# An attention block on one core: the triangular inverse laid out over all row groups of the array, its tiles in three sets, and a reciprocal in two halves

## The chip, the cores and the metric

The kernel runs on one core of a Trainium2 chip. A core has five engines that run side by side, each in the order of its own program: PE (TensorE: matmuls into PSUM, with its weight loads shown apart as PEld), DVE (VectorE), ACT (ScalarE), POOL (GpSimd), and SP (SyncE), which here only issues DMA transfers. The metric is the device time of one execution in microseconds (us). Three runs of the kernel before took 3192.85, 3196.23 and 3197.49 us.

## The reference

Input x is 4 x 512 x 512 in f32 (4 batches, 512 tokens, 512 channels). Two layers are added to it. The first is a gated recurrence over tokens (called wkv below) whose result feeds a gated delta-rule attention with 16 query/key heads and 32 value heads of 128; the second is another wkv, followed by a 512 x 512 product with a binarized weight:

```python
x = x + attn(wkv(x, fside, fside, w1, u1, cond), W_qkvz, W_ba, conv_w, dt_bias, A_log, norm_w, W_out)
x = x + ffn(wkv(x, fside, fside, w2, u2, cond), weight, bias)
```

Of wkv, what matters here is its end, in which a forward and a backward scan over the tokens are divided by each other:

```python
num = nf + nb - ekv + euk * vf
den = df + db - ek + euk
base = sigmoid(r) * (num / maximum(den, 1e-08))
```

Of the attention, what matters is the inverse of a triangular matrix for each chunk of tokens and each value head, and its use:

```python
M = where(stril, einsum('bhncd,bhnmd->bhncm', k_beta, k) * decay, 0.0)
T = solve_triangular(eye + M, eye, lower=True)
v_c = einsum('bhnij,bhnjd->bhnid', T, v_beta)
```

The kernel computes this with chunks of 128 tokens, so that T is a 128 x 128 matrix, and a unit of work has 8 of them.

## The kernel before, in words

**Units.** The attention is cut into 64 units, one for each batch and query/key head (`unit`, L164: batch `n // 16`, head `n % 16`). A unit has two value heads and four chunks of 128 tokens, so NM = 8 triangular matrices. Weights come from HBM raw in the first batch, are turned on PE and stored for the three other batches.

**The plan.** The main loop runs once for each unit, and in each iteration goes through a list of 22 places (`plan`, L1027 to L1097), counted here from 0 to 21. Each place names a few steps and the unit that each is for, relative to the iteration: F is the iteration's own unit (projection, convolution, inverse), C the one before it (the chunk recurrence), O the one before that (norm of the output, turning), W the one before that (the product with W_out), and K the one that is six ahead (its keys, and the triangular matrix itself). Every instruction is kept in program order on its engine, so the order of this list is the order on each engine and in SP's queue of DMA issues.

**The recurrence** of unit C takes four rounds through the places: `chunk_r` (PE, tile ps_s, from the state), `chunk_r_end` (DVE, tile r), `chunk_w` (PE, tile ps_w, from r and the inverse), `chunk_w_end` (ACT, tile wd), `chunk_t` (PE, tiles ps_st and ps_o), `chunk_t_end` (DVE, tiles state and o). The fourth round has `chunk_r` at place 16, `chunk_w` at place 18 and `chunk_t` at place 20.

**The inverse.** The diagonal 32 x 32 blocks of each triangular matrix are inverted by substitution on POOL, four units at a time (`group_load`, `group_step`, `group_end`; the last stores them to HBM as `blocks_n` and, turned, as `blocks_t`, at place 13 of every fourth iteration). `inverse_load` (L651) brings a unit's blocks back into two tiles: `inv_t`, 128 partitions x 8 matrices x 128, which becomes the turned inverse, and `inv_n`, 64 partitions x 8 x 96. There are two sets of these tiles, used in turn, so the load for unit F + 1 stands behind the last `chunk_w` of unit C, at place 20. It is 7 DMA issues. Four steps on PE then put the off-diagonal blocks together, each followed by a copy from PSUM on DVE:

- step 1, `inverse_1` at place 2: 16 products of 32 x 32 blocks. The operands stand in partitions 32 to 63 or 96 to 127; the results go to PSUM partitions 0 to 31 or 32 to 63. The copy makes tile nv, 64 x 256.
- step 2, `inverse_2` at place 4: 24 products of 32 x 32 blocks, with operands in partitions 0 to 31, 32 to 63 and 0 to 31 in turn, and results in partitions 0 to 31, 64 to 95 and 32 to 63. Three copies of 32 x 256 put them into `inv_t` and `inv_n`.
- step 3, `inverse_3` at place 8: 8 products of 64 x 64 blocks, operands in partitions 64 to 127, results in 0 to 63. The copy makes tile nw, 64 x 512.
- step 4, `inverse_4` at place 10: 8 products of 64 x 64 blocks, operands and results in partitions 0 to 63. One copy of 64 x 512 into `inv_t`.

A product takes its row group of the array from the partitions of its operands, and its column group from the partitions of its result. All four steps, and also `key_pairs` (tile ps_kk, place 16) and `queries` (tile ps_kq, place 20), use the one PSUM bank with the tag "inv": each has to wait until what was in the bank has been read. For `queries` this is the end of `key_matrix` (L588; DVE, tile dkd, four operations at place 17 and four at place 18). In the profile a product of f32 shows as two matmul rows, so step 1 has 32 of them, step 2 has 48, and steps 3 and 4 have 16 each; ps_i is the tile of steps 1 and 3, ps_j that of steps 2 and 4.

**The wkv pieces.** The wkv of later batches, and all of the second wkv, are cut into 28 pieces of 128 channels x 512 tokens. A piece rides along in an iteration (steps named "wkv" in the plan), in those whose unit has the head 3, 4, 5 or 7 (first wkv, batches 0 to 2, for the batch to come) and 9, 11, 12 or 13 (second wkv, all batches). `wkv_over` (L291) is one reciprocal of 128 x 512 on DVE at place 15, ahead of `chunk_r_end` of the fourth round; `wkv_end` (L294) at place 18 uses it, and in the second wkv issues a store (`base2`). At head 8 of the first three batches the gates of the next batch are computed.

**SP's queue** from place 15 on: the load of `wo`, the store of `base2` where there is one, the load for the matrix of unit K + 1 (tile dkd), a weight load, the four stores of `key_blocks` (`blocks_m`), the seven of `inverse_load`, the load of tile dkt, and the next weights.

Before the loop, `inverse_load` is called for units 0 and 1 (L1317, L1318); iteration 0 leaves it out (L1409).

Of the kernel before, what the change touches and what calls it, by code (L numbers as in the profile page):

```python
# [9 lines left out]
F32 = mybir.dt.float32  # L10
# [6 lines left out]
P = 128  # L17
EPS = 1e-6

BS = 32  # L20
# [20 lines left out]
def kernel(  # L41
# [21 lines left out]
    B, S, D = x.shape  # L63
# [29 lines left out]
    def bank(tag, name):  # L93
        return pp.tile([P, 512], F32, tag=tag, name=name, bufs=banks[tag])
# [10 lines left out]
        out=tri_le, in_=tri_le, compare_op=ALU.is_ge, fill=0.0, base=0,  # L105
# [5 lines left out]
        out=tri_gt, in_=tri_gt, compare_op=ALU.is_gt, fill=0.0, base=0,  # L111
# [5 lines left out]


    inv_t, inv_n = [], []
    for i in range(2):  # L120
        t = const.tile([P, NM, P], F32, name=f"inv_t{i}")
        G.memset(t, 0.0)
        inv_t.append(t)
        t = const.tile([2 * BS, NM, 3 * BS], F32, name=f"inv_n{i}")
        G.memset(t, 0.0)
        inv_n.append(t)

# [4 lines left out]
    nw = const.tile([P, 1], F32, name="nw")  # L132
# [10 lines left out]
    blocks_n = dram.tile([NG, GROUP, NB, NM, BS, BS], F32, name="blocks_n")  # L143
    blocks_t = dram.tile([NG, GROUP, NB, NM, BS, BS], F32, name="blocks_t")

    with ExitStack() as main:
# [9 lines left out]
        u1p = main.enter_context(tc.tile_pool(name="u1", bufs=1))  # L156
# [7 lines left out]
        def unit(n):  # L164

            return (*divmod(n, HQ), units.setdefault(n, {}))
# [4 lines left out]
        for cb in range(KT):  # L171
            at = slice(cb * P, (cb + 1) * P)
# [472 lines left out]

        b0, b1, b2, b3 = (slice(d * BS, (d + 1) * BS) for d in range(NB))
        lo, hi = slice(0, 2 * BS), slice(2 * BS, 4 * BS)

        def inverse_load(n):  # L651
            b, hq, u = unit(n)
            Tt, Tn = u["Tt"], u["Tn"] = inv_t[n % 2], inv_n[n % 2]
            g, i = divmod(n, GROUP)
            for d, at in enumerate((b0, b1, b2, b3)):
# [12 lines left out]
        def inverse_1(n):  # L668
            b, hq, u = unit(n)
            M, Tt = u["d"], u["Tt"]  # L670
            ps = u["i"] = by_matrix(f"ps_i_{n}")
            for m in range(NM):
                for to, up, dn in ((b0, b0, b1), (b1, b2, b3)):
                    T.matmul(
                        ps[to, m, :BS], lhsT=M[dn, m, up], rhs=Tt[dn, m, dn], start=True, stop=True
                    )

        def inverse_1_end(n):
            b, hq, u = unit(n)
            u["nv"] = u1p.tile([2 * BS, NM, BS], F32, tag="nv", name=f"nv_{n}")  # L680
            V.tensor_copy(u["nv"], u["i"][lo, :, :BS])
# [13 lines left out]

        def inverse_2_end(n):
            b, hq, u = unit(n)
            Tt, Tn, ps = u["Tt"], u["Tn"], u["i"]
            V.tensor_copy(Tt[b2, :, b3], ps[b2, :, :BS])
            V.tensor_copy(Tn[b1, :, b0], ps[b1, :, :BS])  # L700
            V.tensor_copy(Tt[b0, :, b1], ps[b0, :, :BS])

        def inverse_3(n):
            b, hq, u = unit(n)
            ps = u["i"] = by_matrix(f"ps_i4_{n}")
            for m in range(NM):
                T.matmul(
                    ps[lo, m, :], lhsT=u["d"][hi, m, lo], rhs=u["Tt"][hi, m, hi],
                    start=True, stop=True,
                )  # L710

        def inverse_3_end(n):
            b, hq, u = unit(n)
            u["nw"] = u1p.tile([2 * BS, NM, 2 * BS], F32, tag="nw", name=f"nw_{n}")
            V.tensor_copy(u["nw"], u["i"][lo])

        def inverse_4(n):
            b, hq, u = unit(n)
            ps = u["i"] = by_matrix(f"ps_j4_{n}")
            for m in range(NM):  # L720
                T.matmul(
                    ps[lo, m, :], lhsT=u["Tn"][:, m, lo], rhs=u["nw"][:, m, :], start=True, stop=True
                )

        def inverse_4_end(n):
            b, hq, u = unit(n)
            V.tensor_copy(u["Tt"][lo, :, hi], u["i"][lo])


        def turn(n, r):  # L730
# [287 lines left out]
        def last_add(b, c):  # L1018
# [7 lines left out]
        K, F, C, O, W = AHEAD, 0, -1, -2, -3  # L1026
# [87 lines left out]
        for pool, tag, count, shape in (  # L1114
# [3 lines left out]
            for i in range(count):  # L1118
                t = pool.tile(shape, F32, tag=tag, name=f"lent_{tag}_{i}")
# [6 lines left out]
        for pool, tag, shape in ((u1p, "nz", [P, NC, 2, HD]), (u1p, "hT", [P, 2, S])):  # L1126
            t = pool.tile(shape, F32, tag=tag, name=f"lent_{tag}")
# [65 lines left out]
        for cb in range(KT):  # L1193
            w = wkv_start(0, 0, cb)
# [24 lines left out]
        ps = bank("pj", "ps_wba")  # L1219
# [9 lines left out]
        g = {"b": 0}  # L1229
# [122 lines left out]
        for b in range(B - 1):  # L1352
            i = at + 2 + 2 * b
# [98 lines left out]
```

## Time and profile before

| | us |
|---|---|
| median of three runs (lowest, highest) | 3196.23 (3192.85, 3197.49) |
| profiled execution, its own time | 3197.57 |
| its span, first to last instruction | 3195.8 |
| PE busy | 3069.3 (96%) |
| DVE busy | 2044.6 (64%) |
| ACT busy | 1861.6 (58%) |
| POOL busy | 1329.4 (42%) |

What follows is worked out with the profiled execution. In a row of the groups of instructions stand the engine, the operation, the tile written and those read, rows times columns of the array for a matmul, the size out and in, and the count; behind the first bar the group's busy time in us and the mean duration in ns; behind the second bar the idle time of the engine just before them, and what ended it. In the chain of waits a row has a start, a length, and the engine with its tile. Matmuls overlap one another, so the length of a stretch of them is read from start to start, or from the chain, and not from single durations.

### The profile page before, as it was taken

How to read it: one execution, taken by the hardware profiler on the slowest of the kernel's cores; microseconds unless marked ns; L12 is line 12 of the kernel's file. 1: busy time of each engine (PE TensorE's matmuls, PEld its weight loads, DVE VectorE, ACT ScalarE, POOL GpSimd, SP SyncE). 2: the span in 40 equal slices, each digit the busy share in tenths (PEclk: the TensorE clock that was granted, in tenths of full speed). 3: DMA queues.
4: the chain of work that ended last, by engine and by line, in shares of the span. 5: the costliest groups of instructions: out<-in, count | busy, mean ns of one | idle time of the engine just before them, and what ended most of it. 6: DMA issues, size and time to landing. Idle time of an engine off the chain costs nothing.

```text
span 3195.8 us, 57474 instructions
## 1 busy us (share of the span) xinstructions
PE 3069.3 (96%) x20058; PEld 2055.2 (64%) x20058; DVE 2044.6 (64%) x4454; ACT 1861.6 (58%) x5115; POOL 1329.4 (42%) x3042
## 2 busy tenths in 40 slices
PE   6489999999999999999999999999999999999998
PEld 3356766666766666666666666666666666665664
DVE  7545767666655776667655686667755656577542
ACT  2446666666666666556565666556666555655542
POOL 3216354263522646264432646255442515255302
PEclk9689999999999999999999999999999999999999
DMA  3334444444434323332332323323332332333321
GB/s 74 95 87 130 141 127 119 124 125 128 132 109 142 115 59 106 86 96 78 108 102 78 116 86 83 111 77 95 112 92 76 104 86 86 105 90 93 105 83 53
DMA packets 418800, 320.49 MB, mean 100 GB/s; under 512 B 217104, under 2 KB 326160, under 8 KB 418128
## 3 DMA queue, kind: packets, MB, share of 16 engines
q1 hardware_dynamic: 414288, 314.72, 33.6%
q8 instruction: 160, 2.62, 0.3%
q10 hardware_dynamic: 4224, 2.10, 0.2%
q14 instruction: 128, 1.05, 0.1%
HBM read 246.19 MB, written 70.52 MB: 99 GB/s over the span
## 4 chain that ended last, share of the span: by engine, by line
PE 80%; DVE 11%; ACT 3%; DMA 3%; issue 1%; SPq 1%; ACTq 0%; POOL 0%; DVEq 0%; POOLq 0%
PE ps_p L80 24%; PE ps_out L80 12%; PE ps_z L80 12%; PE ps_w L80 4%; PE ps_s L80 4%; PE ps_i L80 3%; PE ps_o L80 3%; PE ps_j L80 3%; DVE y L80 3%; PE ps_st L80 2%; PE ps_kq L80 2%; PE ps_f L80 2%; DVE f L80 2%; PE ps_h L80 1%; PE ps_v L80 1%
## 5 line engine op out<-in xcount | busy, mean ns | idle before, releaser
L80 PE MATMUL ps_p<-cT,w 128*128 128x512 f32 x2000 | 956.4, 606 | 8.4 <-ACT w L80 8.4
L80 DVE SCALAR_TENSOR_TENSOR y<-ps_p,cw,y 128x511 f32<-128x511 f32 (+2 forms) x768 | 570.9, 743 | 419.3 <-ACT y L80 405.6
L80 PEld LDWEIGHTS ps_p<-cT,w 128*128 128x128 f32 x2000 | 346.9, 191 | 302.0 <-issue 270.8
L80 PE MATMUL ps_z<-w,cT 128*128 128x256 f32 x2048 | 476.5, 379 | 0.0
L80 PE MATMUL ps_out<-wo,hT 128*128 128x512 f32 x1024 | 466.8, 599 | 7.3 <-DMA wo<-wosc 7.3
L80 PEld LDWEIGHTS ps_z<-w,cT 128*128 128x128 f32 x2048 | 373.7, 190 | 42.5
L80 PEld LDWEIGHTS ps_out<-wo,hT 128*128 128x128 f32 x1024 | 186.0, 191 | 195.8 <-issue 189.0
L80 POOL TENSOR_TENSOR L<-L,t 128x30 f32<-128x30 f32 (+14 forms) x450 | 270.4, 601 | 35.3
L80 ACT ACT_TABLE_LOAD x137 | 175.8, 1283 | 154.0 <-DVE y L80 116.0
L80 ACT ACTIVATE qs<-ps_s,eg 128x128 f32<-128x128 f32 x384 | 120.5, 366 | 229.5 <-DVE r L80 121.9
L80 POOL TENSOR_TENSOR t<-L 128x30 f32<-128x30 f32 (+14 forms) x450 | 228.7, 508 | 34.5 <-DMA L<-blocks_m 3.3
L80 POOL TENSOR_TENSOR rs_t_o<-rs_y_o 128x8 f32<-128x8 f32 x192 | 38.5, 201 | 461.0 <-DVE rs_y_o L80 450.0
L80 ACT ACTIVATE y<-ps_p,cw 128x512 f32<-128x512 f32 x256 | 174.1, 680 | 90.2 <-PE ps_p L80 90.1
L80 POOL TENSOR_SCALAR_AFFINE_SELECT dkd<-dkd 128x1024 f32<-128x1024 f32 x64 | 70.5, 1101 | 350.4 <-DMA dkd<-gsc 223.0
L80 ACT ACTIVATE dkt<-dkt,gsum 128x128 f32<-128x128 f32 x512 | 162.9, 392 | 69.3 <-POOL dkt L80 68.9
L80 DVE TENSOR_TENSOR x<-x,ps_out 128x512 f32<-128x512 f32 x256 | 168.9, 679 | 32.8 <-PE ps_out L80 32.6
L80 POOL TENSOR_TENSOR rs_t_k<-rs_y_k 128x4 f32<-128x4 f32 x174 | 48.3, 277 | 328.4 <-DVE rs_y_k L80 319.3
L80 DVE SCALAR_TENSOR_TENSOR o<-o,rs_y_o,nz 128x128 f32<-128x128 f32 x512 | 183.0, 412 | 0.1
L80 DVE SCALAR_TENSOR_TENSOR r<-ps_s,nbe,vb 128x128 f32<-128x128 f32 x384 | 115.9, 343 | 96.8 <-PE ps_s L80 96.7
L80 ACT ACTIVATE junk<-o 128x128 f32<-128x128 f32 x512 | 158.0, 309 | 31.8 <-DVE o L80 23.6
L80 DVE TENSOR_TENSOR o<-ps_o,qs 128x256 f32<-128x256 f32 x192 | 80.8, 421 | 144.1 <-PE ps_o L80 136.1
L80 ACT ACTIVATE wd<-ps_w,eg 128x128 f32<-128x128 f32 x384 | 119.7, 364 | 87.8 <-PE ps_w L80 87.5
(270 smaller groups left out, 5771.3 us busy)
## 6 DMA issues: line engine op xcount, KB each, us to landing
w<-wsc SPq DMA_DIRECT2D x288, 256.0 KB, 5.3
dkd<-gsc SPq DMA_DIRECT2D x64, 512.0 KB, 4.7
dkt<-gsc SPq DMA_DIRECT2D x64, 512.0 KB, 4.5
wraw<-in_L_attn_W_qkvz_dram SPq DMA_DIRECT2D x96, 256.0 KB, 3.0
wo<-wosc SPq DMA_DIRECT2D x96, 256.0 KB, 3.8
wsc<-w SPq DMA_DIRECT2D x90, 256.0 KB, 2.1
blocks_m<-dkd SPq DMA_DIRECT2D x256, 32.0 KB, 1.7
L<-blocks_m SPq DMA_DIRECT2D x16, 512.0 KB, 5.5
```

The costliest lines, as they stand in the source:

```text
L80: return lambda *args, **kw: tc.keep_in_program_order(op(*args, **kw))
```

## The change

Five edits, of which the first is the core.

1. The products of the inverse are spread over the array. Matrices 0 to 3 and 4 to 7 form two halves. A list `in_turn` takes a matrix of each half alternately, and the half selects the partitions of the results: 0 to 31 and 32 to 63 for one, 64 to 95 and 96 to 127 for the other in step 1; 0 to 63 and 64 to 127 in steps 3 and 4. In steps 2 and 4 the operands follow their half too. In step 2 the three kinds of products stand one kind after the other (all eight of the first, then of the second, then of the third) where they stood matrix by matrix. The number of products stays.
2. The copies from PSUM follow. nv is 128 x 128 in place of 64 x 256; step 2 is followed by six copies of 32 x 128 in place of three of 32 x 256; nw is 128 x 256 in place of 64 x 512; step 4 is followed by two copies of 64 x 256 in place of one of 64 x 512.
3. `inv_n` is laid out by halves, 128 partitions x 4 x 96, so its loads are six of half the size in place of three: `inverse_load` has 10 DMA issues in place of 7.
4. There are three sets of `inv_t` and `inv_n` in place of two, and `inverse_load` of F + 1 moves from place 20 to place 16, ahead of the store of `base2`, the dkd load and the `key_blocks` stores in SP's queue.
5. `wkv_over` does half of the 512 tokens at a time: the first half at the end of place 16, behind `chunk_r_end` and the taps, the second at the end of place 17, behind the first four operations of `key_matrix`. It stood at place 15.

```diff
-    for i in range(2):
+    for i in range(3):
         t = const.tile([P, NM, P], F32, name=f"inv_t{i}")
...
-        t = const.tile([2 * BS, NM, 3 * BS], F32, name=f"inv_n{i}")
+        t = const.tile([P, NM // 2, 3 * BS], F32, name=f"inv_n{i}")
...
-        def wkv_over(w):
-            V.reciprocal(w["df"], w["df"])
+        def wkv_over(w, half):
+            den = w["df"][:, half * S // 2 : (half + 1) * S // 2]
+            V.reciprocal(den, den)
...
+        HM = NM // 2
+        in_turn = [(h * HM + m, h, m) for m in range(HM) for h in range(2)]
...
-            Tt, Tn = u["Tt"], u["Tn"] = inv_t[n % 2], inv_n[n % 2]
+            Tt, Tn = u["Tt"], u["Tn"] = inv_t[n % 3], inv_n[n % 3]
...
-                    Q.dma_start(
-                        out=Tn[b1 if d else b0, :, at],
-                        in_=blocks_n[g, i, d].rearrange("m i j -> i m j"),
-                    )
+                    for h in range(2):
+                        Q.dma_start(
+                            out=Tn[blocks[2 * h + (d > 0)], :, at],
+                            in_=blocks_n[g, i, d, h * HM : (h + 1) * HM].rearrange("m i j -> i m j"),
+                        )
...
-            for m in range(NM):
-                for to, up, dn in ((b0, b0, b1), (b1, b2, b3)):
+            for m, h, mh in in_turn:
+                for up, dn, to in ((b0, b1, 2 * h), (b2, b3, 2 * h + 1)):
                     T.matmul(
-                        ps[to, m, :BS], lhsT=M[dn, m, up], rhs=Tt[dn, m, dn], start=True, stop=True
+                        ps[blocks[to], mh, :BS], lhsT=M[dn, m, up], rhs=Tt[dn, m, dn],
+                        start=True, stop=True,
                     )
...
-            for m in range(NM):
-                for to, at, col in ((b0, b0, b0), (b2, b1, b2)):
-                    T.matmul(
-                        ps[to, m, :BS], lhsT=Tn[at, m, col], rhs=nv[at, m, :], start=True, stop=True
-                    )
-                T.matmul(
-                    ps[b1, m, :BS], lhsT=nv[b0, m, :], rhs=Tn[b0, m, b0], start=True, stop=True
-                )
+            for what in range(3):
+                for m, h, mh in in_turn:
+                    at, dn = blocks[2 * h], blocks[2 * h + 1]
+                    if what == 0:
+                        to, lhsT, rhs = ps[at, mh], Tn[at, mh, b0], nv[at, mh, :]
+                    elif what == 1:
+                        to, lhsT, rhs = ps[dn, mh], Tn[dn, mh, b2], nv[dn, mh, :]
+                    else:
+                        to, lhsT, rhs = ps[at, HM + mh], nv[at, mh, :], Tn[at, mh, b0]
+                    T.matmul(to[:, :BS], lhsT=lhsT, rhs=rhs, start=True, stop=True)
...
+            for h in range(2):
+                at, dn, ms = blocks[2 * h], blocks[2 * h + 1], slice(h * HM, (h + 1) * HM)
+                V.tensor_copy(Tt[b2, ms, b3], ps[dn, :HM, :BS])
+                V.tensor_copy(Tn[dn, :, b0], ps[at, HM:, :BS])
+                V.tensor_copy(Tt[b0, ms, b1], ps[at, :HM, :BS])
...
+            for m, h, mh in in_turn:
                 T.matmul(
-                    ps[lo, m, :], lhsT=u["d"][hi, m, lo], rhs=u["Tt"][hi, m, hi],
+                    ps[halves[h], mh, :], lhsT=u["d"][hi, m, lo], rhs=u["Tt"][hi, m, hi],
                     start=True, stop=True,
                 )
...
+            for m, h, mh in in_turn:
+                at = halves[h]
                 T.matmul(
-                    ps[lo, m, :], lhsT=u["Tn"][:, m, lo], rhs=u["nw"][:, m, :], start=True, stop=True
+                    ps[at, mh, :], lhsT=u["Tn"][at, mh, lo], rhs=u["nw"][at, mh, :],
+                    start=True, stop=True,
                 )
...
-             (chunk_squares, C, 2), ("wkv", wkv_over), (out_start, O, 1), ("sub", 14, None)],
+             (chunk_squares, C, 2), (out_start, O, 1), ("sub", 14, None)],
...
-             (chunk_q_end, C, 3), ("sub", 15, None)],
+             (chunk_q_end, C, 3), (inverse_load, F + 1), ("wkv", wkv_over, 0), ("sub", 15, None)],
-            [(z_product, C, 0, 0), (turn, F, 3), (key_matrix, K, 0), (silu, F, 0), ("sub", 16, None)],
+            [(z_product, C, 0, 0), (turn, F, 3), (key_matrix, K, 0), (silu, F, 0),
+             ("wkv", wkv_over, 1), ("sub", 16, None)],
...
-             (inverse_load, F + 1), ("sub", 19, None)],
+             ("sub", 19, None)],
```

More of the change, by code (lines that the diff above doesn't have):

```diff
@@ L644, in group_end @@
                 )
-        b0, b1, b2, b3 = (slice(d * BS, (d + 1) * BS) for d in range(NB))
-        lo, hi = slice(0, 2 * BS), slice(2 * BS, 4 * BS)
+        blocks = [slice(d * BS, (d + 1) * BS) for d in range(NB)]
+        b0, b1, b2, b3 = blocks
+        halves = lo, hi = slice(0, 2 * BS), slice(2 * BS, 4 * BS)
+        HM = NM // 2
+        in_turn = [(h * HM + m, h, m) for m in range(HM) for h in range(2)]
         def inverse_load(n):
             b, hq, u = unit(n)
-            Tt, Tn = u["Tt"], u["Tn"] = inv_t[n % 2], inv_n[n % 2]
+            Tt, Tn = u["Tt"], u["Tn"] = inv_t[n % 3], inv_n[n % 3]
             g, i = divmod(n, GROUP)
-            for d, at in enumerate((b0, b1, b2, b3)):
+            for d, at in enumerate(blocks):
                 Q.dma_start(
@@ L679, in inverse_1_end @@
             b, hq, u = unit(n)
-            u["nv"] = u1p.tile([2 * BS, NM, BS], F32, tag="nv", name=f"nv_{n}")
-            V.tensor_copy(u["nv"], u["i"][lo, :, :BS])
+            u["nv"] = u1p.tile([P, HM, BS], F32, tag="nv", name=f"nv_{n}")
+            V.tensor_copy(u["nv"], u["i"][:, :HM, :BS])
         def inverse_2(n):
@@ L698, in inverse_2_end @@
             Tt, Tn, ps = u["Tt"], u["Tn"], u["i"]
-            V.tensor_copy(Tt[b2, :, b3], ps[b2, :, :BS])
-            V.tensor_copy(Tn[b1, :, b0], ps[b1, :, :BS])
-            V.tensor_copy(Tt[b0, :, b1], ps[b0, :, :BS])
+            for h in range(2):
[3 more added lines that the diff above has]
+                V.tensor_copy(Tt[b0, ms, b1], ps[at, :HM, :BS])
         def inverse_3(n):
@@ L705, in inverse_3 @@
             ps = u["i"] = by_matrix(f"ps_i4_{n}")
-            for m in range(NM):
+            for m, h, mh in in_turn:
                 T.matmul(
-                    ps[lo, m, :], lhsT=u["d"][hi, m, lo], rhs=u["Tt"][hi, m, hi],
+                    ps[halves[h], mh, :], lhsT=u["d"][hi, m, lo], rhs=u["Tt"][hi, m, hi],
                     start=True, stop=True,
@@ L713, in inverse_3_end @@
             b, hq, u = unit(n)
-            u["nw"] = u1p.tile([2 * BS, NM, 2 * BS], F32, tag="nw", name=f"nw_{n}")
-            V.tensor_copy(u["nw"], u["i"][lo])
+            u["nw"] = u1p.tile([P, HM, 2 * BS], F32, tag="nw", name=f"nw_{n}")
+            V.tensor_copy(u["nw"], u["i"][:, :HM])
         def inverse_4(n):
@@ L719, in inverse_4 @@
             ps = u["i"] = by_matrix(f"ps_j4_{n}")
-            for m in range(NM):
+            for m, h, mh in in_turn:
+                at = halves[h]
                 T.matmul(
-                    ps[lo, m, :], lhsT=u["Tn"][:, m, lo], rhs=u["nw"][:, m, :], start=True, stop=True
+                    ps[at, mh, :], lhsT=u["Tn"][at, mh, lo], rhs=u["nw"][at, mh, :],
+                    start=True, stop=True,
                 )
@@ L726, in inverse_4_end @@
             b, hq, u = unit(n)
-            V.tensor_copy(u["Tt"][lo, :, hi], u["i"][lo])
+            for h in range(2):
+                V.tensor_copy(u["Tt"][lo, h * HM : (h + 1) * HM, hi], u["i"][halves[h], :HM])
         def turn(n, r):
```

## The prediction

> **What bounds the kernel now.** The page's busy shares and its chain of waits come first, then a window over seven iterations (units 48 to 54) in mid-run.
>
> ```profile
> PE 3069.3 (96%) x20058; PEld 2055.2 (64%) x20058; DVE 2044.6 (64%) x4454; ACT 1861.6 (58%) x5115; POOL 1329.4 (42%) x3042
> PE 80%; DVE 11%; ACT 3%; DMA 3%; issue 1%; SPq 1%; ACTq 0%; POOL 0%; DVEq 0%; POOLq 0%
> ...
> 2397.95:2707.76 309.81, 309.81 (x2073) 207.26 (x2072) 181.42 (x435) 185.57 (x526) 117.11 (x332) 1.00 0.31 91
> ```
>
> In the window PE is busy for all of its 309.81 us, 44.26 us an iteration; DVE, next on a path that PE waits for, is busy 59% of it. PE's stream of work sets the time there, and a microsecond taken from it is gained unless PE then waits. The chain inside one such iteration prices the four steps of the inverse and two groups to hold beside them:
>
> ```profile
> 2473.68 0.62 PE ps_i L80 x32
> 2478.80 0.63 PE ps_j L80 x48
> ...
> 2486.54 1.07 PE ps_i L80 x16
> 2490.83 1.07 PE ps_j L80 x16
> 2491.90 0.36 PE psn L80 x8
> 2502.50 0.89 PE ps_kk L80 x8
> ```
>
> The reader is to see that 48 matmuls of step 2 take no longer than 32 of step 1. Step 1 alternates two pairs of row and column group, step 2 three. So time goes by rounds, 16 of them in both, and a round holds as many matmuls as there are different pairs. The last two lines say the same of column groups: psn, four column groups on the same 128 rows, does its 8 matmuls in 0.36 us, ps_kk on the whole array takes 0.89 us for 8 of the same size (128x128).
>
> Third, the idle time of PE by groups, and DVE's durations:
>
> ```profile
> L80 PE MATMUL ps_i<-inv_t,dkd 32*32 32x32 f32 x2048 | 47.7, 194 | 15.7 <-DMA inv_t<-blocks_t 9.6 <-DVE dkd L80 6.0
> L80 PE MATMUL ps_w<-r,inv_t 128*128 128x128 f32 x768 | 119.7, 279 | 10.9 <-DVE r L80 9.8
> ...
> L80 DVE RECIPROCAL f<-f 128x512 f32<-128x512 f32 x28 | 93.9, 3353 | 0.9
> L80 DVE COPY nw<-ps_i 64x512 f32<-64x512 f32 x64 | 43.0, 671 | 10.2 <-PE ps_i L80 10.2
> L80 DVE COPY nv<-ps_i 64x256 f32<-64x256 f32 x64 | 26.1, 408 | 9.4 <-PE ps_i L80 9.3
> L80 DVE RECIPROCAL beta<-beta 128x128 f32<-128x128 f32 x4 | 3.8, 953 | 0.1
> ```
>
> PE stood 9.6 us for the loads of inv_t and 9.8 us for r.
>
> **The change part by part.**
>
> *Steps 1, 3, 4.* In the timeline step 2's first and last matmul start at 1530.51 and 1531.02: 0.51 us for 16 rounds; the other 0.12 of its 0.63 is getting in and out. Step 1 gets four pairs in place of two, so 8 rounds: 0.12 + 0.255 = 0.375, 0.25 less. Steps 3 and 4 get two in place of one: 1.07 - 0.12 = 0.95, halved, 0.475 less each. No row shows two 64-wide products at once; the bounds are 0 and 0.475 each, and I take the upper end, nearest to psn and step 2. In 64 units: -16.0 and -60.8 us.
>
> *Step 2* loses. Its kinds stand one after another, so only two pairs alternate: 24 rounds, 0.12 + 24/16 x 0.51 = 0.885, 0.255 more, unless the array starts the next kind's pairs while the last of the former run. That first passes of three products start before the first one's second pass (timeline: 1530.51, 1530.52, second passes from 1530.56) shows that some reordering exists, not how deep. Bounds 0 and +16.3 us in all; I take the middle, +8.2.
>
> The Trainium skill speaks against steps 1, 2 and 4 (TensorEngine Tiling (Array Packing), Gotcha 1: PSUM Pressure): different row tiles cannot access the same PSUM bank at once, and all results here go to the one bank. By that rule the sum would be that of the rival "one bank" below. The trace does not bear it out: step 2 before already mixes two row groups into this bank, at 0.51 / 48 = 0.011 us a matmul.
>
> *Copies on DVE.* From 671 and 408 ns: 1.03 ns an element and 145 fixed, so 128 elements take 277. nv -0.13; six of 0.277 for three of 0.417: +0.41; nw -0.26; two of 0.41 for one of 0.674: +0.14. Net +0.16 us a unit, priced at nothing: step 2's copies end 5 us before step 3 starts (2525.6 and 2530.7), nw ends 2.4 us before step 4. Without that cover it would be 64 x 0.16 = 10 us.
>
> *Loads of the inverse.* From place 16 they stand ahead of the base2 store, which waits for wkv_end and stands ahead of every wait of PE for them over 0.25 us: all are in units behind an iteration with a piece of the second wkv (iteration 29: base at 1561.14, inv_t last landed at 1571.25, PE waiting 1.40). The 9.6 us go. Three more issues of 0.49 (their spacing in SP's timeline) are 1.5 us in an SP that waits much of the time. What they now pass in SP's queue, the dkd load, the weights, blocks_m, starts up to 4.9 us later where SP has no slack. Every fourth unit they wait for the blocks_t store (landed 2546.28 for unit 52), so dkd goes out at about 2551 instead of 2545.09 and lands by 2556, before the next iteration masks it at 2560. dkt, behind them before, goes out about 3 us earlier. Before the loop there is no cover: inverse_load(0) and (1) run from 148.78 to 155.56, and the weight load behind them ends PE's longest idle time, 24.02 us, at 158.76. Six more issues of 0.49: +2.9 (bounds 0 and 2.9). The two extra memsets are hidden: POOL is idle from 5.69 to 14.09.
>
> *The reciprocal.* In an iteration without a wkv piece (first line) and in one with (the others), DVE before the fourth round:
>
> ```profile
> 2502.63 0.75 DVE L80 SCALAR_TENSOR_TENSOR y<-ps_p,cw,y 128x511 f32<-128x511 f32 x1 [2.26 <-ACT y L80]
> ...
> 1507.60 3.35 DVE L80 RECIPROCAL f<-f 128x512 f32<-128x512 f32 x1
> 1510.87 0.65 DVE L80 SCALAR_TENSOR_TENSOR y<-ps_p,cw,y 128x511 f32<-128x511 f32 x1
> 1513.39 2.15 DVE L80 SCALAR_TENSOR_TENSOR dkd<-ps_kk,nbr,dkd 128x128 f32<-128x128 f32 x8
> ```
>
> The reciprocal fills 2.26 us in which DVE waits for ACT anyway, and pushes r 1.3 us back (1511.44 for a ps_s at 1508.34; 2503.30 for 2501.47). Moved behind r and the taps it no longer fills that hole. The taps follow ps_s as in the plain iteration (2501.47, taps done 2505.25: 3.78 later), so with ps_s at 1508.34 they end at 1512.12. A half is 953 + 128 x 6.25 = 1.75 us. Half, four key_matrix (1.1), half, four more end about 1517.8, against 1515.54. PE's ps_kq wants the bank at 1517.06: a new wait of 0.75. In the pieces of the first wkv ps_s stands at 1139.45, the end comes at 1148.9, ps_kq (without the present wait for r) at 1148.3: 0.6. In the first batch 8 pieces have 2.5 us of cover, because PE turns W_out between. So 12 x 0.75 + 8 x 0.6 = +13.8 us (bounds 0 and 20 x 0.9 = 18). Behind ps_kq, PE's next product stands 0.8 later; nothing else is late. Gained: r no longer late, 8 x 0.3 (ps_w at 1143.67 for 1143.37) and, in the last stretch, 2.37 and 0.31: -5.1. The rest of r's 9.8 us stands beside the gates, where this edit does nothing.
>
> *The sum.* -16.0 - 60.8 + 8.2 - 9.6 + 2.9 + 13.8 - 5.1 = -66.6. In the gates' iterations and in the last seven units PE waits for others; I leave 2 us of the gain there. 3197.57 - 64.6 = 3133.0; the median stands 1.3 below the profiled run: 3132.
>
> **The rivals.**
>
> *One row group, one product* (3162): step 3's two products stream from the same partitions 64 to 127 and might take turns. For it: no 64-wide pair in the trace. Against: psn. Costs 64 x 0.475 = 30.4.
>
> *One bank* (3187): pairs in different row groups take turns. Step 3 keeps its 30.4, steps 1 and 4 gain nothing, step 2 takes the full 16.3: 3132 + 16.0 + 30.4 + 8.1. Against: step 2's 48 matmuls in 0.51.
>
> *Slower: the halves run in series* (3217). Mechanism: a switch of column halves at every product stops the overlap. Steps 1, 3 and 4 stay at 0.62 and 1.07, step 2 pays 16.3: 3132 + 16.0 + 60.8 + 8.1. Then what is left is the wait of ps_kq and the 2.9 before the loop. It decides once the three steps gain less than 0.3 us a unit (the other terms then sum to 16.3 + 2.9 + 13.8 + 2 - 9.6 - 5.1 = +20.3, over 64 units). For it: nothing alternates two 64-wide halves so far. Against: both lines of the chain read above.
>
> *New waits take a third* (3156): shorter steps bring PE sooner to state, nw, r. Covers in the chain's iteration: state to ps_s 2.7 us in the round with step 3, nw 2.4, r 1.7 behind step 2; the cuts are 0.5 at most. Against, therefore, save in iterations with pieces, where DVE has little room.
>
> *All goes well* (3110): step 2 finds its overlap and ps_kq does not wait: 3132 - 8.2 - 13.8.
>
> **How the numbers follow.** Forecast 0.58 (its own range 3117 to 3150), one row group 0.11, one bank 0.04, series 0.09, new waits 0.07, all well 0.11. The range from 3107 to 3168 holds the forecast, "all well", the two middle rivals. What a measurement can tell from no change is about 0.2%, 6 us. Slower by more has most of the series case: 0.08; within it 0.03 from that case and the upper end of one bank; faster 0.89.
>
> **What would show it.** In the chain of the same iteration: ps_i x32 about 0.38, ps_i x16 and ps_j x16 about 0.6, ps_j x48 between 0.63 and 0.89. An iteration without a piece at 43.2 instead of 44.26. No idle time of ps_i on inv_t. Idle time of ps_kq on DVE dkd, 0.6 to 0.75 a piece. The forecast is wrong if the 64-wide steps stay near 1.07, or if idle time of PE appears behind r, nw or state in iterations without a piece.

## The result and the profile after

The changed kernel takes 3145.31 us (median of four runs, 3141.4 to 3150.3) against 3195.92 us for the kernel before beside it: a ratio of 0.984, with a 95% interval of 0.9826 to 0.9854. It is faster by some 51 us, 13 less than forecast, inside the range.

The page of the kernel after: busy time of each engine, and the chain of waits by engine.

```profile
PE 2991.7 (95%) x20058; PEld 1979.9 (63%) x20058; DVE 2066.1 (66%) x4738; ACT 1861.3 (59%) x5115; POOL 1313.4 (42%) x3044
...
PE 72%; DVE 17%; ACT 8%; issue 2%; DMA 1%; SPq 0%; POOL 0%; ACTq 0%; DVEq 0%; POOLq 0%
```

The span went from 3195.8 to 3143.2 us, 52.6 less. PE's busy time fell by 77.6 us (from 3069.3), its idle time rose by 25.1 (from 116.4 to 141.5, the gaps between its matmuls added up). The chain says the same: PE's share of it fell from 80% to 72%, DVE's rose from 11% to 17%, ACT's from 3% to 8%. PE still sets the time in most places, but where DVE and ACT did not get shorter it now waits for them.

The four steps of the inverse in the chain of waits after, in an iteration without a piece (start, length, engine, tile, matmuls; four records of step 2 are missing in the trace):

```profile
2388.95 0.38 PE ps_i L80 x32
...
2393.83 0.69 PE ps_j L80 x44
...
2401.63 0.61 PE ps_i L80 x16
...
2405.46 0.61 PE ps_j L80 x16
...
2432.11 0.38 PE ps_i L80 x32
```

They took 0.62, 0.63, 1.07 and 1.07 us before. The iteration went from 44.26 to 43.16 us (from the first line to the last). The groups of PE's matmuls, with PE's idle time before each and what ended it:

```profile
L80 PE MATMUL ps_p<-cT,w 128*128 128x512 f32 x2000 | 956.4, 606 | 13.6 <-ACT w L80 13.6
...
L80 PE MATMUL ps_w<-r,inv_t 128*128 128x128 f32 x768 | 118.0, 276 | 9.1 <-DVE r L80 9.1
...
L80 PE MATMUL ps_kq<-q,k 128*128 128x128 f32 x512 | 75.0, 290 | 26.9 <-DVE dkd L80 26.4 <-DVE inv_t L80 0.5
...
L80 PE MATMUL ps_i<-inv_t,dkd 32*32 32x32 f32 x2048 | 29.4, 195 | 6.0 <-issue 6.0
```

The wait of ps_i for the loads of inv_t is gone (9.6 us before). ps_kq, which waited 0.2 us before, waits 26.9, 26.4 of it for dkd. ps_p waits 13.6 us for ACT instead of 8.4; that was not foreseen.

The wait of ps_kq shows how a gain on PE is given back. This is an iteration with a piece of the second wkv, in the timelines after of DVE, of ACT and of PE (start, length, engine, what, and in brackets the idle time before it):

```profile
1479.94 0.42 DVE L80 TENSOR_SCALAR f<-f 128x512 f32<-128x512 f32 x1
1482.29 0.75 DVE L80 SCALAR_TENSOR_TENSOR y<-ps_p,cw,y 128x511 f32<-128x511 f32 x1 [1.93 <-ACT y L80]
1482.95 0.60 DVE L80 SCALAR_TENSOR_TENSOR r<-ps_s,nbe,vb 128x128 f32<-128x128 f32 x2
1483.47 1.52 DVE L80 SCALAR_TENSOR_TENSOR y<-ps_p,cw,y 128x510 f32<-128x510 f32 x2
1484.91 1.74 DVE L80 RECIPROCAL f<-f 128x256 f32<-128x256 f32 x1
1486.57 1.03 DVE L80 SCALAR_TENSOR_TENSOR dkd<-ps_kk,nbr,dkd 128x128 f32<-128x128 f32 x4
1487.51 1.74 DVE L80 RECIPROCAL f<-f 128x256 f32<-128x256 f32 x1
1489.17 1.03 DVE L80 SCALAR_TENSOR_TENSOR dkd<-ps_kk,nbr,dkd 128x128 f32<-128x128 f32 x4
```

```profile
1479.29 0.63 ACT L80 ACTIVATE v<-y 128x512 f32<-128x512 f32 x1 [3.67 <-DVE y L80]
...
1481.59 0.67 ACT L80 ACTIVATE y<-ps_p,cw 128x512 f32<-128x512 f32 x1
```

```profile
1479.92 0.60 PE L80 MATMUL ps_s<-state,k 128*128 128x256 f32 x2
...
1488.28 0.43 PE L80 MATMUL psn<-sq,ones 128*32 128x128 f32 x8
1490.26 1.16 PE L80 MATMUL ps_kq<-q,k 128*128 128x128 f32 x8 [1.55 <-DVE dkd L80]
```

PE's ps_s stands at 1479.92. ACT stood 3.67 us for DVE's taps before it came to v, so its y ends 2.34 us behind ps_s (1481.59 + 0.67). DVE waited 1.93 us for that y; its first tap starts 2.37 us behind ps_s, where the forecast had 1.16. From there DVE is busy without a gap to the end of the last key_matrix at 1490.2, while PE was through with psn at 1488.7: it stood for 1.55 us. In the iteration shown of before, ps_s was at 1508.34 and ACT's y done at 1509.46, only 1.12 behind (timelines before, of PE and of ACT):

```profile
1508.34 0.60 PE L80 MATMUL ps_s<-state,k 128*128 128x256 f32 x2
```

```profile
1508.79 0.67 ACT L80 ACTIVATE y<-ps_p,cw 128x512 f32<-128x512 f32 x1
```

Shorter steps made PE some 1.2 us earlier, and nothing made DVE and ACT, which wait for each other here, any earlier.

### The profile page after: what moved, and what is told of

It reads as the page before. It is cut to its first block, busy times and chain, and to the rows that moved or that the text cites. A ratio compares the mean times of both kernels' runs of the same rounds, so it can differ in the third digit from the quotient of the medians.

```text
span 3143.2 us, 57926 instructions
## 1 busy us (share of the span) xinstructions
PE 2991.7 (95%) x20058; PEld 1979.9 (63%) x20058; DVE 2066.1 (66%) x4738; ACT 1861.3 (59%) x5115; POOL 1313.4 (42%) x3044
## 3 DMA queue, kind: packets, MB, share of 16 engines
q14 instruction: 131, 1.07, 0.1%
## 4 chain that ended last, share of the span: by engine, by line
PE 72%; DVE 17%; ACT 8%; issue 2%; DMA 1%; SPq 0%; POOL 0%; ACTq 0%; DVEq 0%; POOLq 0%
PE ps_p L80 20%; PE ps_out L80 13%; PE ps_z L80 11%; DVE y L80 5%; PE ps_w L80 4%; PE ps_s L80 4%; PE ps_o L80 3%; PE ps_kq L80 2%; PE ps_st L80 2%; DVE f L80 2%; PE ps_f L80 2%; PE ps_j L80 2%; PE ps_i L80 1%; PE ps_v L80 1%; ACT y L80 1%
## 5 line engine op out<-in xcount | busy, mean ns | idle before, releaser
L80 PE MATMUL ps_p<-cT,w 128*128 128x512 f32 x2000 | 956.4, 606 | 13.6 <-ACT w L80 13.6
L80 POOL TENSOR_TENSOR L<-L,t 128x30 f32<-128x30 f32 (+14 forms) x450 | 248.7, 553 | 34.9
L80 POOL TENSOR_TENSOR rs_t_k<-rs_y_k 128x4 f32<-128x4 f32 x174 | 55.8, 321 | 348.5 <-DVE rs_y_k L80 339.4
L80 ACT ACTIVATE v<-y 128x512 f32<-128x512 f32 x128 | 80.7, 630 | 203.6 <-DVE y L80 201.0
L80 DVE SCALAR_TENSOR_TENSOR o<-o,rs_y_o,nz 128x128 f32<-128x128 f32 x512 | 189.8, 428 | 1.2 <-POOL rs_y_o L80 1.2
L80 DVE TENSOR_TENSOR x<-x,ps_out 128x512 f32<-128x512 f32 x256 | 168.9, 679 | 25.1 <-PE ps_out L80 24.9
L80 ACT COPY w<-ps_w 128x256 f32<-128x256 f32 (+1 forms) x346 | 145.4, 431 | 46.6 <-PE ps_w L80 46.4
```

Source lines behind the costliest of these rows:

```text
L80: return lambda *args, **kw: tc.keep_in_program_order(op(*args, **kw))
```

## The experiments

The runs were made in three groups, each beside the kernel before: recip_back, recip_fill, spread_only and recip_only (before: 3193.33 us), load_back, half_major, step2_order and fill_and_order (3194.52), store_behind and store_behind_fill (3193.75). Unless a diff is against the kernel before, it is against the changed kernel. Expectations are quoted as they were written ahead of the runs.

**Where the reciprocal stands.** Two kernels differ from the changed one in `wkv_over` alone.

recip_back has the whole reciprocal at place 15, as before:

```diff
...
-             (chunk_squares, C, 2), (out_start, O, 1), ("sub", 14, None)],
+             (chunk_squares, C, 2), ("wkv", wkv_over), (out_start, O, 1), ("sub", 14, None)],
...
-             (chunk_q_end, C, 3), (inverse_load, F + 1), ("wkv", wkv_over, 0), ("sub", 15, None)],
+             (chunk_q_end, C, 3), (inverse_load, F + 1), ("sub", 15, None)],
...
-             ("wkv", wkv_over, 1), ("sub", 16, None)],
+             ("sub", 16, None)],
```

> The changed kernel with the reciprocal whole and at place 15 again. Theory of the prediction: PE's gain in the inverse stands by itself, and the wait of ps_kq comes from the reciprocal's new place alone; then the 26 us of it go, r is late as before the change by a few us in all, and the time is 3145 - 26 + 5 = about 3124. Rival theory: in iterations with a wkv piece DVE and ACT have a pace of their own, PE is now 1.1 us ahead of them, and gives that back where it next meets them; then the wait moves from ps_kq to ps_w (for r): with the reciprocal ending at 1483.7 in the iteration that starts its fourth round at 1479.92, r ends at 1484.9 and ps_w, due at 1483.84, waits about 1.05 us in pieces of the second wkv, and about 1.7 in those of the first (their extra operation of 0.7 stands ahead of the reciprocal); some 25 us in all, and the time stays at 3141 to 3148.

recip_fill has the first half at place 15 and the second behind the last key_matrix, at place 18 (its places 16 and 17 are those of recip_back):

```diff
-             (chunk_squares, C, 2), (out_start, O, 1), ("sub", 14, None)],
+             (chunk_squares, C, 2), ("wkv", wkv_over, 0), (out_start, O, 1), ("sub", 14, None)],
...
-             (turn_end, F, 3), (square, F, 0), (key_matrix, K, 1), ("wkv", wkv_end),
+             (turn_end, F, 3), (square, F, 0), (key_matrix, K, 1), ("wkv", wkv_over, 1), ("wkv", wkv_end),
```

> The changed kernel with the first half of the reciprocal at place 15, where DVE waits about 1.9 us for ACT before the tap, and the second half at place 18 behind the last key_matrix, just ahead of wkv_end. Both theories: the first half (1.74 us) lies in that idle time, key_matrix ends at about taps + 2.15, that is 1487.1 in the iteration where ps_kq is due at 1488.64, so no wait of ps_kq; r is late by 0 to 0.2 us. 3145 - 25 = about 3120. If the rival theory holds in its strong form (PE gives back its lead wherever it meets DVE), waits of another kind of about 1 us a piece come up in its place (ps_w for r, or the next iteration's ps_st and ps_s), and the time is 3135 or more.

recip_back took 3141.35 us (ratio 0.9833, 0.9817 to 0.985), recip_fill 3119.09 us (0.9766, 0.9747 to 0.9784). The same two groups of PE, first of recip_back, then of recip_fill:

```profile
L80 PE MATMUL ps_w<-r,inv_t 128*128 128x128 f32 x768 | 120.6, 280 | 28.1 <-DVE r L80 28.1
...
L80 PE MATMUL ps_kq<-q,k 128*128 128x128 f32 x512 | 75.0, 290 | 0.5 <-DVE inv_t L80 0.5
```

```profile
L80 PE MATMUL ps_w<-r,inv_t 128*128 128x128 f32 x768 | 118.4, 277 | 8.9 <-DVE r L80 8.9
...
L80 PE MATMUL ps_kq<-q,k 128*128 128x128 f32 x512 | 75.0, 290 | 0.5 <-DVE inv_t L80 0.5
```

With the reciprocal ahead of r, PE waits for r (28.1 us); with it behind r but ahead of key_matrix, PE waits for dkd (26.4) and for r only 9.1. Most of the wait only moved (26.4 us at dkd became 19 more at r), so the order within these places was not what cost most of the time: DVE's work up to the last key_matrix, counted from ACT's y, was longer than PE's. In recip_fill the first half runs in the 1.93 us that DVE waits for y, and the second when PE has what it needs. The waits that the pieces brought are gone from both groups (the 8.9 us left for r stand beside the gates and in the last units), and 26 us with them.

**What each edit is worth without the others.** spread_only keeps edits 1 to 3 with two sets of tiles, the loads at place 20 and the whole reciprocal at place 15. recip_only is the kernel before with edit 5 alone. load_back is the changed kernel with the loads at place 20. The loads' move alone on the kernel before was not tried, as it needs a third set of the larger tiles of that kernel.

spread_only (its reciprocal as in recip_back):

```diff
-    for i in range(3):
+    for i in range(2):
...
-            Tt, Tn = u["Tt"], u["Tn"] = inv_t[n % 3], inv_n[n % 3]
+            Tt, Tn = u["Tt"], u["Tn"] = inv_t[n % 2], inv_n[n % 2]
...
-             (chunk_q_end, C, 3), (inverse_load, F + 1), ("wkv", wkv_over, 0), ("sub", 15, None)],
+             (chunk_q_end, C, 3), ("sub", 15, None)],
...
-             ("sub", 19, None)],
+             (inverse_load, F + 1), ("sub", 19, None)],
```

> The kernel before with the spread inverse alone (its copies and its layout of inv_n with 10 loads included): two sets of tiles, loads at place 20, one reciprocal at place 15. An iteration without a piece: 43.16 us. Theory of the prediction: -70 from PE, nothing else: 3126 plus the 2.9 before the loop = 3129. Rival theory: 20 pieces give back 1 to 1.7 us each at ps_w for r (25 us), and the waits for inv_t stay or grow, since PE comes to them 1.1 us sooner (10 to 20 us): 3153 to 3170.

recip_only, against the kernel before:

```diff
...
-             (chunk_squares, C, 2), ("wkv", wkv_over), (out_start, O, 1), ("sub", 14, None)],
+             (chunk_squares, C, 2), (out_start, O, 1), ("sub", 14, None)],
...
-             (chunk_q_end, C, 3), ("sub", 15, None)],
+             (chunk_q_end, C, 3), ("wkv", wkv_over, 0), ("sub", 15, None)],
...
+             ("wkv", wkv_over, 1), ("sub", 16, None)],
```

> The kernel before with the reciprocal in two halves at places 16 and 17, and nothing else. This prices the move where PE has its old pace. Theory of the prediction (its sum on DVE): ps_kq waits 0.75 us in pieces of the second wkv and 0.6 in those of the first, in batches from 1 on, 14 us in all, r gains up to 5: 3196 + 9 = 3205. If the sum on DVE itself was wrong, the wait is 1.5 here as in the changed kernel, 27 us in all: 3218. If the pace of DVE and ACT is what made the wait long in the changed kernel, it is 0.6 to 0.75 here.

load_back:

```diff
-             (chunk_q_end, C, 3), (inverse_load, F + 1), ("wkv", wkv_over, 0), ("sub", 15, None)],
+             (chunk_q_end, C, 3), ("wkv", wkv_over, 0), ("sub", 15, None)],
...
-             ("sub", 19, None)],
+             (inverse_load, F + 1), ("sub", 19, None)],
```

> The changed kernel with inverse_load at place 20 again, three sets kept. If the loads' place was worth what the prediction said, idle time of ps_i for inv_t of about 10 us comes back, more if PE, 1.1 us earlier in each iteration, meets the loads sooner (up to 20): 3155 to 3165. If the third set alone was what freed the loads, or the waits were hidden behind others, the time stays at 3145.

All three came out slower than expected. Together with the others they fill a table:

| products | reciprocal at place | loads at place | us | PE idle on inv_t loads |
|---|---|---|---|---|
| before | 15 | 20 | 3193.33 to 3195.92 | 9.6 |
| before | 16 and 17 (recip_only) | 20 | 3229.37 (ratio 1.0109, 1.0094 to 1.0125) | 24.0 |
| spread | 15 (spread_only) | 20 | 3190.46 (0.9987, 0.9977 to 0.9998) | 25.9 |
| spread | 16 and 17 (load_back) | 20 | 3227.87 (1.0105, 1.0091 to 1.0119) | 43.3 |
| spread | 15 (recip_back) | 16 | 3141.35 (0.9833, 0.9817 to 0.985) | 0 |
| spread | 16 and 17 (after) | 16 | 3145.31 (0.984, 0.9826 to 0.9854) | 0 |

With the loads at place 20, spreading the products gains next to nothing (rows 1 and 3, 2 and 4), though each iteration without a piece is 1.10 us shorter there too (43.16): those behind a piece of the second wkv are longer (the one from step 3 of unit 25 to that of unit 26 went from 44.26 to 48.56 in spread_only). Moving the reciprocal costs 36 to 37 us there. With the loads at place 16 the two differ by 4 us, and their intervals overlap. The loads' move, priced at 9.6 us, is worth 49 us beside a whole reciprocal (rows 3 and 5) and 83 beside the halves (rows 4 and 6).

recip_only also prices the wait of ps_kq at PE's old pace. half_major (below) does so too: its iterations without a piece are as long as before, but its reciprocal and its loads stand as in the changed kernel. PE's group in recip_only, then in half_major:

```profile
L80 PE MATMUL ps_kq<-q,k 128*128 128x128 f32 x512 | 75.0, 290 | 5.9 <-DVE dkd L80 5.8 <-DVE inv_t L80 0.2
```

```profile
L80 PE MATMUL ps_kq<-q,k 128*128 128x128 f32 x512 | 75.0, 290 | 12.6 <-DVE dkd L80 12.2 <-DVE inv_t L80 0.5
```

In each kernel these are 17 waits for dkd: of 0.34 us in recip_only (its expectation had 0.6 to 0.75 for this case), of 0.54 to 0.90 in half_major, and of 1.55 in the changed kernel. So the reciprocal's new place alone costs a small wait, and PE's lead over DVE and ACT (1.2 us in the iteration above) makes it long.

Two things make the loads' move worth so much. First the wait itself. SP's queue in load_back, around the start of a unit behind an iteration with a piece of the second wkv (timeline: start, length, and the transfer issued):

```profile
2215.53 0.60 SPq L80 DMA_DIRECT2D wo<-wosc  x1
2227.01 0.32 SPq L80 DMA_DIRECT2D base<-ek  x1
2227.45 0.36 SPq L80 DMA_DIRECT2D dkd<-gsc  x1
2227.85 0.45 SPq L80 DMA_DIRECT2D w<-wsc  x1
2228.35 2.07 SPq L80 DMA_DIRECT2D blocks_m<-dkd  x4
2230.46 0.48 SPq L80 DMA_DIRECT2D inv_t<-blocks_t  x1
...
2235.18 0.43 SPq L80 DMA_DIRECT2D inv_t<-blocks_t  x1
```

SP stands from 2216.1 to 2227.0 for `wkv_end`, whose result the store of base2 (base in the trace) carries. All that is queued behind the store goes out one by one, 0.4 to 0.5 us each, and the loads of the inverse come after six others, from 2230.5 to 2235.6. PE began step 1 at 2234.25 and stood 2.61 us in it. Every microsecond by which PE is earlier or `wkv_end` later lengthens this wait.

Second, the clock. Here are busy times and, behind those of the five engines, the granted clock of the same stretch (then the DMA share and GB/s):

```profile
2234.00:2236.00 2.00, 0.35 (x4) 0.14 (x2) 1.31 (x4) 2.00 (x8) 0.00 (x0) 1.00 0.30 47
2236.00:2237.00 1.00, 0.00 (x0) 0.00 (x0) 0.00 (x0) 0.29 (x1) 0.00 (x0) 0.71 0.31 70
2237.00:2243.00 6.00, 5.93 (x40) 3.29 (x41) 2.02 (x6) 2.39 (x9) 1.09 (x1) 0.50 0.89 296
2243.00:2244.00 1.00, 1.00 (x4) 0.46 (x3) 0.00 (x0) 0.17 (x2) 0.00 (x0) 0.88 0.15 35
2244.00:2250.00 6.00, 6.00 (x67) 3.37 (x66) 4.53 (x15) 2.87 (x10) 0.00 (x0) 1.00 0.50 133
```

For 6.8 us, from about 2236.4 to 2243.2, PE had half the clock. PE was at work from 2237.07, so 3.1 us were lost on top of the 2.61 of the wait. Added over the whole span, the missing share of the clock is 57 us in the changed kernel (mean granted clock 0.982), all of it before 251 us or after 2844, and 80 in load_back (0.975), 27 of them between 642 and 2295 us. The 23 us between the two are close to the 25.1 by which PE's busy time is longer in load_back (3016.8 against 2991.7 us). With 52.9 us of further idle time that makes 78.0 of the 78.2 us between the two spans. So in load_back the added waits cost PE about half as much again as the trace shows as idle time.

**What holds the loads.** store_behind is load_back with the store of base2 issued behind the loads, still at place 20 (the diff is against load_back); store_behind_fill has the reciprocal of recip_fill on top of it.

```diff
-            if n == 1:
-                Q.dma_start(out=base2[b, cb], in_=num)
+        def wkv_store(w):
+            if w["n"] == 1:
+                Q.dma_start(out=base2[w["b"], w["cb"]], in_=w["nf"])
...
-             (inverse_load, F + 1), ("sub", 19, None)],
+             (inverse_load, F + 1), ("wkv", wkv_store), ("sub", 19, None)],
```

> load_back (the changed kernel with the loads at place 20, 3227.87 us) with one more edit: the store of base2 is issued behind the loads of the inverse instead of ahead of them. In load_back SP stood from 2216.13 to 2227.01 us for the store (it waits for wkv_end on DVE, done 2226.98) and issued the loads 3.4 us behind it, 2230.46 to 2235.6; they landed 2.6 us after PE wanted them. Theory 'the store holds the queue': without it SP waits only for key_matrix (done about 2226.3), the dkd and weight loads go out before that, and the loads of the inverse start about 2 us sooner. Of the 38 us of waits behind a store some 26 go, and with them most of the 24 us lost to the halved clock that followed the long ones: 3175 to 3195 us. Rival 'the place itself is too late, the store is one of several waits': 3215 us or more.

> store_behind with the reciprocal placed as in recip_fill (first half at place 15, second half behind the last key_matrix). Theory 'what counts is when DVE ends key_matrix': its end comes some 3.5 us sooner, the stores of blocks_m and the loads behind them go out before PE needs them although they stand at place 20, and the time is that of recip_fill, 3117 to 3130 us. Rival 'the loads need the early place': 3150 us or more.

store_behind took 3172.48 us (ratio 0.9933, 0.9917 to 0.995), store_behind_fill 3126.64 (0.9788, 0.9773 to 0.9802). PE's first step, in load_back, store_behind and store_behind_fill:

```profile
L80 PE MATMUL ps_i<-inv_t,dkd 32*32 32x32 f32 x2048 | 35.6, 199 | 51.5 <-DMA inv_t<-blocks_t 43.3 <-issue 6.0 <-DVE x L80 1.1
```

```profile
L80 PE MATMUL ps_i<-inv_t,dkd 32*32 32x32 f32 x2048 | 33.9, 195 | 17.7 <-DMA inv_t<-blocks_t 11.4 <-issue 6.0
```

```profile
L80 PE MATMUL ps_i<-inv_t,dkd 32*32 32x32 f32 x2048 | 31.2, 195 | 7.7 <-issue 6.0 <-DMA inv_t<-blocks_t 1.4
```

The wait for the loads falls from 43.3 to 11.4 us with nothing changed but the order of one store and ten loads, and PE's busy time falls with it, from 3016.8 to 2997.7, as the clock stays up (59 us missing in place of 80). That is 55 us of the 83 (the forecast for it, 3175 to 3195, was a little too high). With key_matrix earlier as well, the wait is down to 1.4 us and the loads do no harm at place 20. So it was the queue behind the store, and DVE's lateness in front of it, that the early place got rid of; beyond that the place itself is worth some 8 us (3126.64 against 3119.09), and the intervals overlap.

**The order of the products.** half_major takes the four matrices of one half first and then those of the other, so that the same pair of row and column group repeats.

```diff
-        in_turn = [(h * HM + m, h, m) for m in range(HM) for h in range(2)]
+        in_turn = [(h * HM + m, h, m) for h in range(2) for m in range(HM)]
```

> The changed kernel with the matrices of one half first and then those of the other, in all four steps, in place of alternating; the same products at the same places. If matmuls are taken in order with a short look-ahead (about 3 rounds, from step 2's 0.69 where 0.885 was the sum without any), the halves run one after the other: step 1 (16 - 3) rounds, 0.53 us; steps 3 and 4 about 0.9 each; step 2 48 - 15 = 33 rounds, 1.17. That is 1.2 us more an iteration: 3205 to 3222, worse than before the change. If the array takes matmuls of different groups out of a deep queue in any order, or if the gain came from the partitions and not from the alternation, the time stays at 3145.

step2_order goes matrix by matrix in step 2, with the three kinds and the two halves in turn. These six products use four pairs of row and column group, since the first and the third kind have the same two.

```diff
-            for what in range(3):
-                for m, h, mh in in_turn:
+            for mh in range(HM):
+                for what, h in ((0, 0), (0, 1), (1, 0), (1, 1), (2, 0), (2, 1)):
```

> The changed kernel with step 2 going matrix by matrix, its three kinds and two halves inside, in place of kind by kind; the same 24 products. If time goes by rounds of different pairs of row and column group, pairs (0,0) and (2,2) have 8 products each in any order, so 16 rounds: ps_j x48 takes 0.63 us in place of 0.69, 64 x 0.06 = 4 us less in an iteration's sum, a little less in the time (3141 to 3143). If the queue of matmuls already overlapped the kinds as far as it can, nothing changes; if the order kind by kind was faster, 0.75 or more.

half_major took 3194.06 us (ratio 1.0, 0.9991 to 1.0009), step2_order 3146.91 (0.985, 0.9836 to 0.9864). The steps in the chains of the two kernels (some records are missing here too):

```profile
2383.81 0.53 PE ps_i L80 x30
...
2388.83 1.13 PE ps_j L80 x48
...
2397.07 0.89 PE ps_i L80 x16
...
2401.18 0.89 PE ps_j L80 x16
```

```profile
2400.71 0.62 PE ps_j L80 x42
...
2408.45 0.61 PE ps_i L80 x16
...
2412.27 0.61 PE ps_j L80 x16
```

In half_major the same products in the same places of the array take 0.53, 1.13, 0.89 and 0.89 us; the iteration without a piece is back at 44.31 us, and the whole gain is gone. So products overlap because they alternate; where they lie is not enough. The steps came out as the expectation had worked them out from a queue that looks some three rounds ahead. The time is 11 us below its 3205 to 3222, as the slower PE waits less: its idle time is 21.6 us shorter than in the changed kernel, with ps_kq at 12.6 in place of 26.9. In step2_order step 2 takes 0.62 in place of 0.69 (the expectation had 0.63 for 16 rounds), and that iteration 43.09 in place of 43.16 us; the time of the kernel can't be told from that of the changed one, as its interval overlaps. The 0.07 us were not given back to the named waits (ps_kq 26.9, r 9.2); the 2 us longer wait of ps_p for ACT is part of it, and the rest stays open.

**The two that gained, together.** fill_and_order is recip_fill with step 2 of step2_order.

> The changed kernel with both edits: the first half of the reciprocal at place 15, the second at place 18, and step 2 matrix by matrix. Sum of the two: 3145 - 25 - 3 = about 3117. If the pieces give the gain back elsewhere, 3135 or more.

It took 3115.68 us (3113.31 to 3117.18; ratio 0.9756, 0.9743 to 0.9769), faster than both kernels, and 30 us below the changed one. The 3.4 us between it and recip_fill lie within the intervals.

## Why the prediction came out as it did

- *Steps 1, 3 and 4, -76.8.* Right in mechanism and size: 0.38, 0.61 and 0.61 us for 0.375, 0.595 and 0.595. Step 3, whose two products stream from the same partitions and differ in column group alone, gained as much as step 4: the rival "one row group" is out. So is "one bank": in step 4 two row groups write to one bank, and overlap. The Trainium skill (TensorEngine Tiling (Array Packing), Gotcha 1: PSUM Pressure) says that this can't be; these runs do not bear it out for f32 products that write to different partitions of the bank.
- *Step 2, +8.2.* It cost 0.06 us a unit, 3.8 in all; the array starts the next kind's pairs early, nearly as the lower bound had it. The model of rounds holds in step2_order too: two of its four pairs have eight products each, which makes 16 rounds in any order, 0.63 us, and it took 0.62.
- *Halves in series.* Ruled out. Its mechanism is the wrong way round: the switch of halves at every product is what makes the overlap, and half_major, which switches once in a pass, loses most of it: an iteration is 0.05 us longer than before, and the kernel takes 3194 us. The rival's 3217 had 0.26 us an iteration (13 us more in 64); the other 10 were not taken apart.
- *ps_kq, +13.8.* This is the term that was mis-sized: 17 waits of 1.55 us, 26.4 in all. The prediction took the taps' distance from ps_s out of an iteration without a piece. With a piece, the distance was the same before (y done 1.12 us behind ps_s) only because PE was no faster than DVE and ACT there; what PE gained in the four steps it then had to wait. At PE's old pace the 17 waits are of 0.34 us (recip_only) or 0.54 to 0.90 (half_major), about what the forecast had; the rest of the 1.55 is PE's lead. It also counted three pieces too many: those of the last batch at heads 11, 12 and 13 ride in iterations that have no unit K, so no key_matrix stands there, and 17 pieces wait where 20 were priced.
- *r, -5.1.* It fell by 1.8 (10.9 to 9.1): the waits beside the gates stay and the eight small ones go, as forecast (they show as 0.14 us each, where the forecast had 0.3), but in the last stretch 2.37 and 0.31 only became 1.36 and 0.65.
- *"New waits take a third".* It was said to hold in iterations with pieces alone, and there it did. The 5.2 us of ps_p on ACT's w, in the first batch's iterations with pieces (up to 0.88 each), belong to it too. The time lies between the forecast and this rival.
- *The loads, -9.6.* The idle time went, every bit. But its price was that of the kernel before; in the changed kernel the same move is worth 49 to 83 us, as the table shows. The sum came out because all five edits were in it, though its parts could not have been bought one by one.
- *Before the loop, +2.9.* Right: the longest idle time went from 24.02 to 26.68 us. *Copies, nothing:* right; the nv, step 2 and nw copies measure 282, 286 and 409 ns, and the waits of ps_j for them do not grow.
- *The sum.* Forecast -64.6, measured -52.6 on the span. -70.4 for the steps (64 x 1.10), -9.6, +2.7, +26.4, -1.8, +5.2 make -47.5; PE's busy time fell by 7 us more than the 70.4, at the start and by 0.1 to 0.2 us in iterations with a wait, which no step had and whose cause is open; other waits took 2 back. So waits cost some 21 us more than forecast (12.6 for ps_kq, 3.3 for r, 5.2 for ps_p), and 9 us more than forecast came off PE's own work. Of these, the 7 that no step had are luck.

## What to carry to other kernels

A term of a sum holds for the kernel that it was read in. Before an engine is made faster, look at every transfer it will meet sooner: if that transfer stands in a queue behind a store that waits for another engine, the gain is spent there, so move the load first and take the gain second. And when a second engine already runs at the pace of the first, moving its work to and fro within one stretch only moves the wait; put the work into the holes where that engine waits itself, or behind the last thing that the first one needs.

## What the runs showed of the hardware

- After some waits of PE in mid-run the granted clock went to 0.50, for 6.8 us in the windows of load_back above, for about 3.4 us after eight of the 14 waits for inv_t in spread_only. The halved stretches in the traces of this case last 3.4 us or a whole multiple of it, but for those that the end of a trace cuts off. In load_back it followed eight of the ten waits for inv_t of over 2.5 us; in spread_only one of only 1.79 (2119.47). It followed none of the 17 waits of 1.55 in the changed kernel, nor one of 2.84 in the kernel before (1480.10). The same wait of 2.5 us for r beside the gates lost the clock in spread_only (1303.43) and not in the changed kernel (1282.56). The Trainium skill has such a gate (TensorE: Matmul & The Clock Gate, "Why this matters for your kernels"): no idle gaps over some 3 us between bursts of matmuls. The mechanism agrees; the length is shorter here, and doesn't decide alone. By the same page of the Trainium skill ("What's actually happening") the gate looks at windows that run free of the kernel. That where in a window a gap falls decides here is a guess from that; no run shows it.
- Products that differ in column group alone overlap when they alternate (16 matmuls of 64 x 64 in 0.61 us in place of 1.07), and much less when four products of one column group stand in a row (half_major, 0.89).
